# A mixture-of-experts layer with cross attention: another order of the first rows' work, and the second v and W of later rows between gate products

## The chip, the cores and the metric

One core of one Trainium2 chip runs the kernel. The metric is the device time of one execution in microseconds; the time before is the median of three runs. TensorE's granted clock was full (1.0) throughout the profiled execution.

## The reference

Eight batch rows of 512 tokens with 256 channels, and for each a context of 64 tokens. All is float32.

```python
nx = _layer_norm(x, ln_gamma, ln_beta)
q = nx @ Wq
k = prototype_bank @ Wk
v = prototype_bank @ Wv
scores = jnp.einsum('bth,bph->btp', q, k) * H ** (-0.5)
weights = jax.nn.softmax(scores, axis=-1)
evidence = jnp.einsum('btp,bph->bth', weights, v)
combined = jnp.concatenate([nx, evidence, anchor], axis=-1)
router_probs = jax.nn.softmax(combined @ router_W + router_b, axis=-1)
h = jax.nn.silu(jnp.einsum('btc,ecr->bter', combined, e_w1) + e_b1)
expert_out = jnp.einsum('bter,erh->bteh', h, e_w2) + e_b2
routed = jnp.sum(expert_out * router_probs[..., None], axis=-2)
g = jax.nn.sigmoid(jax.nn.silu(combined @ gate_w1 + gate_b1) @ gate_w2 + gate_b2)
return x + g * (routed @ out_w + out_b)
```

There are three experts of 512 hidden channels; `anchor` is one vector for each batch row.

## The kernel before

The batch rows are taken in four pairs, j = 0 to 3. For a pair the kernel runs `gate_layer`, then `expert_layer` for e = 0, 1, 2, then `outputs`. The text calls pair 0 "the first rows". The order of all instructions on every engine is the order in which the program writes them (`manual_schedule`); semaphores between engines follow from who reads and writes which tile.

**Seven products for eight.** The two batch rows of a pair, the two halves of the 256 input channels and neighbouring chunks of 128 output channels make 2x2 block products, which are done with seven products (`nx_product`, which = 1 to 7) over sums and differences of the blocks. The differences of the weights (`ws`, called sums in the text) are made once on GpSimd: `combine_weights(g)` is four adds or subtracts (L233 to L236) for expert g, with g = E for the gate. The differences of x (t1 to t4) are made by `combine_x` (L640). Products are accumulated in PSUM banks U, Y and Z, with L792 as the line of all of them; partial results are copied out by ScalarE (`keep_part`, L834) and added by VectorE (`add`, L831). A product that accumulates in U can start only when the copy before it has read U.

**Evidence.** The context part of `combined` is not formed. `value_weights(j, g)` multiplies v with the middle third of expert g's first weights ("v and W", `vw`, four matmuls at L767, a copy at L774), and `evidence` multiplies the turned softmax weights `wT` with it, as two streams on the two halves of the array. `value_differences` (L781) subtracts neighbouring chunks of `vw` for one of the two batch rows. Expert 0 and the gate need theirs at the end of `gate_layer`; expert 1's ("the second v and W") is used at the end of expert 0's layer.

**PSUM.** Eight banks. The small jobs take theirs from a list in turn (`misc`, set by `spares`): before the loop banks 4, 6, 7, in `gate_layer` 7 and 5. A bank is free again when what was in it has been read.

**The first rows.** Before the loop the program lists one by one: context and weights turned, v, keys joined with queries (`project(wkqT, ...)`, copied by `keep_m`, L360 and L361), x normalized and turned by TensorE (`transpose_x`, scaled on the way out by VectorE L566 for the first half of the channels and by ScalarE L570 for the second), the scores (L649), the softmax (L659 to L686: transposed, maximum, subtract, exp, sum, reciprocal, multiply), and `turn_weights` (L693, L695). `anchor_rows(g)` multiplies the anchors with the last third of the weights; `anchor_columns` adds the biases later. `load_table` runs a dummy activation, so that the table of a function is loaded at that place in ScalarE's queue.

**GpSimd's queue** carries, besides the sums, DMAs of the router: `store_router_rows` (two stores to `vrd`), `store_router_anchor` (`rbd`, from `scr_k`), `spread_router_bias` (two loads of `rbd`, L407), `spread_router_rows` (two loads of `vrd`, L423), and `router_column` (two multiplies or subtracts, L402 and L403). SyncE's queue loads all weights, in order; `load_second(0)` (L475) is the load of the first expert's second weights into a buffer that held `rrow`, the source of the `rbd` store.

**Later rows.** While `outputs(j)` runs its long products (`experts`), steps for pair j + 1 are put between them, by the dictionary `between`; those for a layer itself are in `within`. The points are names: P2, P7, P3 and so on lie between two calls of `experts`, "gate" between products 3 and 7 of `gate_layer`, (0, "S") after the first silus of expert 0's layer, (0, "A"), (0, "B"), (0, "C"), (0, "D") further down in it.

Of the kernel before, what the change touches and what calls it, by code (L numbers as in the profile page):

```python
# [9 lines left out]
AF = mybir.ActivationFunctionType  # L10
# [6 lines left out]
def kernel(  # L17
# [100 lines left out]
    def load_table(func):  # L118
        nc.scalar.activation(warm_t, warm_t, func)
# [254 lines left out]
    def router_anchor():  # L374
        ps = misc("ps_rb")
        for k in range(KH):
            nc.tensor.matmul(
                ps[:ED, :B], rwd[:, 2 * KH + k, :], condT[:, k, :B], start=(k == 0), stop=False
            )
        for k in range(KH):  # L380

            nc.tensor.matmul(
                ps[:ED, :B], rw2[:, k, :ED], beta_c[:, k : k + 1].to_broadcast([P, B]),
                start=False, stop=(k == KH - 1),
            )
        dst = rrow.rearrange("e (i j) -> e j i", i=2)
        src = ps[:ED, :B].rearrange("e (j i) -> e j i", i=2)
        nc.scalar.activation(dst, src, AF.Identity, bias=rb_c[:, 0:1])
# [253 lines left out]
    def scores(j):  # L642


        ps = misc(f"ps_s_{j}")
        for g in range(2):
            for k in range(KH):
                for i, h in SIDES:
                    nc.tensor.matmul(  # L649
                        ps[side(i, h), g * NH : (g + 1) * NH],  # L650
                        mr[:, k, 2 * j + i, g * TB : (g + 1) * TB],
                        S["nxT", 2 * j + i][:, k, h * NH : (h + 1) * NH],
                        start=(k == 0),
                        stop=(k == KH - 1),
                    )
        w = work.tile([P, 2, NJ, TB], F32, tag="w", name=f"w_{j}", bufs=1)
        S["w", j] = w
        tokens = w.rearrange("p g j c -> p j g c")
        nc.vector.transpose(w.rearrange("p g j c -> p (g j c)"), ps)  # L659
        nc.vector.tensor_copy(logits(j)[:, 1, :], w[:, 0, :, 0])  # L660
        nc.vector.memset(w[:, 0, :, 0], 0.0)
        mx = work.tile([P, NJ], F32, tag="mx", name=f"mx_{j}")
        nc.vector.tensor_reduce(mx, tokens, AX.XY, ALU.max)
        sm = work.tile([P, NJ], F32, tag="sm", name=f"sm_{j}")
        S["sm", j] = sm
        if j == 0:
            nc.vector.tensor_tensor(w, w, by_token(mx), ALU.subtract)
            nc.scalar.activation(w, w, AF.Exp, scale=SCALE)
            nc.vector.tensor_reduce(sm, tokens, AX.XY, ALU.add)
            return  # L670
        nmx = work.tile([P, NJ], F32, tag="nmx", name=f"nmx_{j}")
        nc.vector.tensor_scalar_mul(nmx, mx, -SCALE)
        for t in range(NJ):
            nc.scalar.activation(
                w[:, :, t, :], w[:, :, t, :], AF.Exp, bias=nmx[:, t : t + 1], scale=SCALE,
                accum_out=sm[:, t : t + 1],
            )

    def by_token(a):
        return a.unsqueeze(1).unsqueeze(3).to_broadcast([P, 2, NJ, TB])  # L680
# [527 lines left out]
    with tc.manual_schedule(engines=None):  # L1208
# [33 lines left out]
        load_table(AF.Exp)  # L1242
        project(wkqT, ctxT, keep_m, "m")
        router_anchor()
        value_weights(0, E)
        store_router_rows(0)
        store_router_anchor()
        combine_weights(E)
        transpose_x(1)
        combine_x(0, nc.vector, (0, 1))  # L1250
        scores(0)
        load_table(AF.Silu)
        combine_weights(0)
        router_column()
        spread_router_bias()
        spread_router_rows(0)
        softmax(0)
        value_weights(0, 0, nc.vector.tensor_copy)
        anchor_rows(E)
        anchor_rows(0)  # L1260
        combine_x(0, nc.vector, (2,))
        turn_weights(0)
        combine_weights(1)
        late_scratch()
        load_anchor(1)
        load_anchor(2)
# [4 lines left out]
        for j in range(NP):  # L1271


            within, between = {}, {}

            def put(where, n, step, *args):
                where.setdefault(n, []).append(lambda: step(*args))

            if j == 0:
                put(within, "gate", value_weights, 0, 1)  # L1280
                put(within, (0, "S"), combine_x, 0, nc.vector, (3,))
                put(within, (0, "S"), router_part, 0)
                put(within, (0, "A"), router_part, 1)
                put(within, (0, "A"), load_x, 2)
                put(within, (0, "A"), load_x, 3)
                put(within, (0, "B"), combine_weights, 2)
                put(within, (0, "B"), combine_gate)
                put(within, (0, "A"), anchor_rows, 1)
                put(within, (0, "A"), router_logits, 0)
                put(within, (0, "A"), load_second, 1)  # L1290
                put(within, (0, "C"), transpose_second, 0)
                put(within, (0, "C"), anchor_columns, 1)
                put(within, (0, "C"), anchor_rows, 2)
                put(within, (0, "C"), second_bias)
                put(within, (0, "C"), router_exp, 0)
                put(within, (0, "D"), router, 0)
                put(within, (0, "C"), load_second, 2)
                put(within, (0, "D"), second_layer, 0)
                put(within, (0, "D"), spread_probabilities, 0)
                put(within, (0, "D"), combine_second, 0)  # L1300
                put(within, (1, "A"), transpose_second, 1)
                put(within, (1, "B"), second_layer, 1)
                put(within, (1, "B"), combine_second, 1)
                put(within, (1, "C"), transpose_second, 2)
                put(within, (1, "C"), anchor_columns, 2)
                put(within, (1, "D"), second_layer, 2)
                put(within, (1, "D"), combine_second, 2)
            if j:
                put(within, (0, "S"), router, j)
                put(within, (0, "S"), spread_probabilities, j)  # L1310
            if j and j + 1 < NP:
                put(within, (0, "B"), statistics, 2 * j + 3, 0, NT)
            put(within, (0, "C" if j == 0 else "B"), value_weights, j, 2)
            put(within, (1, "C"), load_x_blocks, 2 * j)
            put(within, (2, "A"), gate_differences, j)
            put(within, (2, "C"), load_x_blocks, 2 * j + 1)
            if j + 1 < NP:
                b0, b1 = 2 * j + 2, 2 * j + 3
                if j + 2 < NP:
                    put(between, "begin", load_x, b0 + 2)  # L1320
                    put(between, "begin", load_x, b1 + 2)
                put(within, (0, "A" if j else "D"), statistics, b0, 0, NT)
                if j == 0:
                    put(within, (0, "D"), statistics, b1, 0, NT)
                for i in range(2):
                    put(within, (0, "D") if j else (1, "S"), deviation, j + 1, i)
                for b in (b0, b1):
                    put(within, (1, "W" if j else "S"), normalize, b)
                    put(within, (1, "W" if j else "S"), store_x, b)
                put(within, (1, "C"), regroup_x, b0)  # L1330
                put(within, (1, "A" if j else "B"), router_part, b0)
                put(within, (1, "D" if j else "B"), router_part, b1)
                put(between, "begin", transpose_blocks, b0)
                put(between, "gate", regroup_x, b1)
                put(between, "begin", value_weights, j + 1, E)
                put(between, "begin", store_router_rows, j + 1)
                put(between, "begin", spread_router_rows, j + 1)
                put(between, "P5", transpose_blocks, b1)
                put(between, "P2", scores, j + 1)
                put(between, "P2", combine_x, j + 1, nc.gpsimd)  # L1340
                put(between, "P7", softmax, j + 1)
                put(between, "P7", value_weights, j + 1, 0)
                put(between, "P7", router_logits, j + 1)
                put(between, "P3", value_weights, j + 1, 1)
                put(between, "P3", turn_weights, j + 1)
                put(between, "P3", router_exp, j + 1)
            gate_layer(j, within)
            for e in range(E):
                expert_layer(j, e, within)
            outputs(j, between)  # L1350
# [34 lines left out]
```

## Time and profile before

| | us |
|---|---|
| median of 3 runs (lowest, highest) | 465.32 (464.8, 465.38) |
| the profiled execution, its own time | 465.82 |
| its span, first to last instruction | 463.7 |
| TensorE busy | 458.4 |
| VectorE busy | 365.9 |
| ScalarE busy | 214.3 |
| GpSimd busy | 101.0 |

A row of a timeline has: start in us from the span's start, time in us (of all instructions of the row, if there are several), engine, line, operation, what it writes and reads, shape, count, and in brackets the idle time of the engine before it with what ended it. PE is TensorE's matmul, PEld its weight load, DVE VectorE, ACT ScalarE, POOL GpSimd, SPq SyncE's queue. A row of the chain of waits in order of time has start, time, engine, tile and line. The ends of matmuls are modelled, so matmul starts are the safer numbers. A row of the waits has who waited, for whom, total us, times, longest.

### The profile page before, as it was taken

The numbers are of one execution on the slowest core, as the hardware profiler recorded it, in microseconds if no ns is written. First come the engines' busy times: TensorE is split into PE (matmuls) and PEld (weight loads), VectorE is DVE, ScalarE is ACT, GpSimd is POOL, SyncE is SP. The second block draws the span as 40 slices with busy tenths as digits, with TensorE's granted clock in tenths as the row PEclk, the third lists the DMA queues.
The fourth block names the chain that finished last, engine by engine and source line by source line (L and its number), as shares of the span: only waits on it lengthen the run. The fifth ranks groups of instructions, "written<-read, shape, count | busy, mean of one in ns | idle before, by whom it ended". The sixth has DMA issues, their size and how long they took to land.

```text
span 463.7 us, 4758 instructions
## 1 busy us (share of the span) xinstructions
PE 458.4 (99%) x1457; PEld 210.0 (45%) x1457; DVE 365.9 (79%) x683; ACT 214.3 (46%) x370; POOL 101.0 (22%) x149
## 2 busy tenths in 40 slices
PE   9999999999999999999999999999999999999996
PEld 7534555444444444444444444444444444444455
DVE  2898878969799659879799659978889625797983
ACT  3435583656222566557221576458230455458000
POOL 6475614101081300001072300001062300000020
PEclk9999999999999999999999999999999999999999
DMA  8983677402012325812011334702011480000014
GB/s 280 371 167 102 100 234 114 98 0 45 7 23 39 65 104 128 149 41 46 6 24 23 46 136 107 112 9 46 6 24 23 70 205 0 0 0 1 0 19 72
DMA packets 119401, 35.26 MB, mean 76 GB/s; under 512 B 106045, under 2 KB 116337, under 8 KB 118865
## 3 DMA queue, kind: packets, MB, share of 16 engines
q1 hardware_dynamic: 115168, 26.95, 28.7%
q0 software_dynamic: 2176, 7.17, 4.7%
q10 hardware_dynamic: 2032, 0.85, 0.7%
q8 instruction: 11, 0.18, 0.2%
q14 instruction: 14, 0.11, 0.1%
HBM read 27.56 MB, written 7.39 MB: 75 GB/s over the span
## 4 chain that ended last, share of the span: by engine, by line
PE 93%; DVE 6%; issue 0%; ACT 0%
PE ps_u L792 42%; PE ps_z L792 18%; PE ps_y L792 13%; PE ps_vw L767 5%; PE ps_gu L792 3%; PE ps_w2o L501 2%; PE ps_s L649 2%; PE ps_gz L792 1%; DVE h L1068 1%; PE ps_tokens L792 1%; PE ps_wake L294 1%; DVE h L876 1%; PE ps_v L339 1%; PE ps_m L339 1%; PE ps_gy L792 1%; DVE r L1078 0%
## 5 line engine op out<-in xcount | busy, mean ns | idle before, releaser
L876 DVE TENSOR_TENSOR h<-h,pb 128x512 f32<-128x512 f32 x96 | 62.0, 696 | 6.5 <-ACT h L825 6.5
L792 PE MATMUL ps_u<-h,w2o 128*128 128x512 f32 x144 | 64.1, 594 | 0.0
L792 PE MATMUL ps_u<-nxT,w 128*128 128x512 f32 x112 | 55.5, 606 | 0.0
L825 ACT ACTIVATE h<-h,abias 128x512 f32<-128x512 f32 x72 | 49.6, 719 | 12.5 <-DVE h L831 12.0
L1101 POOL TENSOR_TENSOR yb<-yb,xb 128x512 f32<-128x512 f32 x14 | 18.4, 1318 | 145.5 <-DVE yb L1100 128.2
L792 PE MATMUL ps_z<-wT,vw 64*128 64x512 f32 x104 | 49.5, 605 | 0.0
L792 PE MATMUL ps_z<-h,w2s 128*128 128x512 f32 x96 | 42.6, 593 | 0.2 <-DVE r L1084 0.2
L792 PEld LDWEIGHTS ps_u<-h,w2o 128*128 128x128 f32 x144 | 27.0, 190 | 32.5 <-issue 29.7
L834 ACT COPY h<-ps_u 128x512 f32<-128x512 f32 x48 | 28.0, 582 | 29.7 <-PE ps_u L792 29.4
L415 POOL DMA_DIRECT2D vrd<-vw x8 | 5.0, 629 | 137.1 <-ACT vw L774 137.1
L1068 DVE TENSOR_TENSOR h<-h,h 128x1024 f32<-128x1024 f32 x24 | 34.4, 1487 | 0.0
L792 PEld LDWEIGHTS ps_u<-nxT,w 128*128 128x128 f32 x112 | 19.9, 189 | 30.1 <-issue 25.6
L825 ACT ACTIVATE h<-ps_u,abias 128x512 f32<-128x512 f32 x24 | 16.5, 687 | 29.7 <-PE ps_z L792 29.4
L831 DVE TENSOR_TENSOR h<-h,ps_y 128x512 f32<-128x512 f32 x24 | 16.4, 683 | 17.2 <-PE ps_y L792 15.7
L792 PEld LDWEIGHTS ps_z<-h,w2s 128*128 128x128 f32 x96 | 18.1, 190 | 23.5 <-issue 21.8
L792 PE MATMUL ps_z<-T,ws 128*128 128x512 f32 x56 | 28.6, 592 | 0.0
L792 PE MATMUL ps_y<-nxT,w 128*128 128x512 f32 x56 | 28.6, 592 | 0.0
L792 PE MATMUL ps_u<-wT,vw 64*128 64x512 f32 x56 | 27.9, 613 | 0.5 <-DVE hg L831 0.5
L831 DVE TENSOR_TENSOR h<-h,ps_z 128x512 f32<-128x512 f32 x24 | 16.2, 685 | 14.2 <-PE ps_z L792 14.1
L792 PE MATMUL ps_y<-wT,vw 64*128 64x512 f32 x56 | 27.0, 596 | 0.0
L767 PE MATMUL ps_vw<-w,vT 128*128 128x512 f32 (+1 forms) x64 | 27.0, 544 | 0.0
L792 PE MATMUL ps_u<-T,ws 128*128 128x512 f32 x56 | 26.8, 595 | 0.1
(236 smaller groups left out, 804.2 us busy)
## 6 DMA issues: line engine op xcount, KB each, us to landing
pb<-pd POOLq DMA_DIRECT2D x4, 1536.0 KB, 6.4
xb<-in_x_dram SPq DMA_DIRECT2D x64, 64.0 KB, 2.5
out_dram<-yb SPq DMA_DIRECT2D x56, 64.0 KB, 2.0
w<-in_L_xcond_e_w_dram SPq DMA_DIRECT2D x6, 512.0 KB, 10.3
x<-in_x_dram SPq DMA_DIRECT2D x24, 128.0 KB, 3.0
xd<-x SPq DMA_DIRECT2D x24, 128.0 KB, 2.4
xg<-xd SPq DMA_DIRECT2D x48, 64.0 KB, 2.4
scr_wa<-in_L_xcond_e_w_dram SPq DMA_DIRECT2D x3, 512.0 KB, 16.6
```

The lines of the kernel that those rows point to most:

```text
L339: nc.tensor.matmul(ps, w_sb[:, k, m * P : (m + 1) * P], src[:, k, :], start=(k == 0), stop=(k == KH - 1))
L415: nc.gpsimd.dma_start(S["vrd", j][i].rearrange("e c -> c e"), S["vw", j][row_half(i), R0:])
L501: nc.tensor.matmul(ps[:, d * H : (d + 1) * H], w2T[:, k, (i + d) * P : (i + d + 1) * P], ow_sb[:, k, :], start=(k == 0), stop=(k == KH - 1),)
L649: nc.tensor.matmul(ps[side(i, h), g * NH : (g + 1) * NH], mr[:, k, 2 * j + i, g * TB : (g + 1) * TB], S["nxT", 2 * j + i][:, k, h * NH : ( ...
L767: nc.tensor.matmul(ps, vT[:, k, j * 2 * CT : (j + 1) * 2 * CT], w1[:, KH + k, n0:n1], start=(k == 0), stop=(k == KH - 1),)
L792: nc.tensor.matmul(ps, lhsT, rhs, start=start, stop=True, skip_group_check=not start)
L825: nc.scalar.activation(h, h if src is None else src, AF.Silu, bias=abias[:, c, 2 * j + i : 2 * j + i + 1])
L831: nc.vector.tensor_tensor(h, h, part, ALU.add)
L834: nc.scalar.copy(chunk(n, i, d), part)
L876: nc.vector.tensor_tensor(h, h, S["pb", j][:, i, :, 2 * q // RC, :], ALU.mult)
L1068: nc.vector.tensor_tensor(d, p, m, ALU.subtract)
L1101: nc.gpsimd.tensor_tensor(yb, yb, S["xb", 2 * j + row][:, i, :], ALU.add)
```

## The change

In the first rows:

- x of the second batch row is turned before the gate's v and W is multiplied, instead of after it.
- The sum over the exponentials becomes a step of its own (`sum_weights`), which stands after the anchor rows.
- The first v and W is copied by ScalarE instead of VectorE, and its difference follows after the softmax.
- The load of the Silu table moves from behind the scores to the "gate" point, behind the second v and W.
- On GpSimd, `router_column` and `spread_router_bias` go ahead of `combine_weights(0)`, and `combine_weights(1)` moves from before the loop to point (0, "B") of the first expert layer.
- The second v and W's difference moves from the "gate" point to (0, "S").

In the later rows the second v and W moves from point P3 of the outputs before to the "gate" point between products 3 and 7, and its difference to (0, "S").

```diff
@@ scores
             nc.scalar.activation(w, w, AF.Exp, scale=SCALE)
-            nc.vector.tensor_reduce(sm, tokens, AX.XY, ALU.add)
             return
@@ new
+    def sum_weights(j):
+        nc.vector.tensor_reduce(
+            S["sm", j], S["w", j].rearrange("p g j c -> p j g c"), AX.XY, ALU.add
+        )
@@ before the loop
         router_anchor()
+        transpose_x(1)
         value_weights(0, E)
         store_router_rows(0)
         store_router_anchor()
         combine_weights(E)
-        transpose_x(1)
         combine_x(0, nc.vector, (0, 1))
         scores(0)
-        load_table(AF.Silu)
-        combine_weights(0)
         router_column()
         spread_router_bias()
+        combine_weights(0)
         spread_router_rows(0)
-        softmax(0)
-        value_weights(0, 0, nc.vector.tensor_copy)
+        value_weights(0, 0, nc.scalar.copy, False)
         anchor_rows(E)
         anchor_rows(0)
+        sum_weights(0)
+        softmax(0)
+        value_differences(0, 0)
         combine_x(0, nc.vector, (2,))
         turn_weights(0)
-        combine_weights(1)
         late_scratch()
@@ in the loop, j == 0
-                put(within, "gate", value_weights, 0, 1)
+                put(within, "gate", value_weights, 0, 1, nc.scalar.copy, False)
+                put(within, "gate", load_table, AF.Silu)
                 put(within, (0, "S"), combine_x, 0, nc.vector, (3,))
+                put(within, (0, "S"), value_differences, 0, 1)
                 put(within, (0, "S"), router_part, 0)
...
+                put(within, (0, "B"), combine_weights, 1)
                 put(within, (0, "B"), combine_weights, 2)
@@ in the loop, j > 0
             if j:
+                put(within, "gate", value_weights, j, 1, nc.scalar.copy, False)
+                put(within, (0, "S"), value_differences, j, 1)
                 put(within, (0, "S"), router, j)
...
                 put(between, "P7", router_logits, j + 1)
-                put(between, "P3", value_weights, j + 1, 1)
                 put(between, "P3", turn_weights, j + 1)
```

## The prediction

> **What bounds the kernel now.** I read the busy shares first, then the chain of waits, then the timeline of the first 37 us and of the start of the second pair of rows.
>
> ```profile
> PE 458.4 (99%) x1457; PEld 210.0 (45%) x1457; DVE 365.9 (79%) x683; ACT 214.3 (46%) x370; POOL 101.0 (22%) x149
> ...
> PE 93%; DVE 6%; issue 0%; ACT 0%
> ```
>
> TensorE carries 93% of the chain that ended last. So an edit pays only where it closes a gap between two products. In the chain in order of time a product of 512 columns (two instructions) takes 0.86 us and the four of a v-times-W product take 1.72:
>
> ```profile
> 43.98 0.86 PE ps_y L792 x2
> ...
> 132.95 1.72 PE ps_vw L767 x4
> ```
>
> With those two prices I compared each stretch with what it would take without gaps. After 37 us almost nothing is left except the steps between tile shapes (about 0.1 us each, in every pair of rows). The gaps that this change can reach lie in four places.
>
> Scores of the first rows. L649 begins at 19.63; its second rows' part waits until VectorE has written the turned x (L566, end 20.11), a loss of 0.08 us:
>
> ```profile
> 18.32 0.68 DVE L361 TENSOR_TENSOR mr<-ps_m,scr_small 128x504 f32<-128x504 f32 x1
> 19.30 0.81 DVE L566 TENSOR_SCALAR nxT<-pt_x,cols 128x512 f32<-128x512 f32 x1 [0.30 <-PE pt_x L579]
> 19.63 2.46 PE L649 MATMUL ps_s<-nxT,mr 128*32 128x256 f32 x32
> 20.17 0.16 PEld L649 LDWEIGHTS ps_s<-nxT,mr 128*32 128x32 f32 x8 [0.39 <-DVE nxT L566]
> ```
>
> First gate layer. The table load keeps ScalarE until 26.98, so its copy out of U ends at 27.55 and product 6, which adds to U, starts at 27.70:
>
> ```profile
> 24.73 1.12 PE L792 MATMUL ps_u<-nxT,w 128*128 128x512 f32 x2
> 25.58 1.28 ACT L119 ACT_TABLE_LOAD   x1
> 26.98 0.57 ACT L834 COPY hg<-ps_u 128x512 f32<-128x512 f32 x1
> 27.67 0.30 PEld L792 LDWEIGHTS ps_u<-T,ws 128*128 128x128 f32 x2 [0.92 <-POOL w L235]
> ```
>
> The row names L235, but that ended at 26.98 and belongs to another expert's sums; what ended just before is the copy. From 24.73 to the first evidence product at 32.16 are 7.43 us. Six products and one v-times-W are 6x0.86+1.72 = 6.88, and two shape steps 0.19: 7.07. **Gap 0.36.**
>
> First evidence. The last turning of the softmax weights ends at 32.51, so the two half-array streams run out of step; then the next evidence product needs U, and the sum that reads U (L831) queues behind the difference of the second v and W (L781):
>
> ```profile
> 32.16 0.69 PE L792 MATMUL ps_y<-wT,vw 64*128 64x512 f32 x1
> 33.34 0.91 DVE L781 TENSOR_TENSOR vw<-vw 64x256 f32<-64x256 f32 x1
> 34.28 0.69 DVE L831 TENSOR_TENSOR hg<-hg,ps_u 128x512 f32<-128x512 f32 x1
> 35.02 0.18 PEld L792 LDWEIGHTS ps_u<-wT,vw 64*128 64x128 f32 x1 [1.31 <-DVE hg L831]
> 36.94 1.12 PE L792 MATMUL ps_u<-nxT,w 128*128 128x512 f32 x2
> ```
>
> The same stretch of the second rows, and the fourth gap ahead of it:
>
> ```profile
> 146.52 1.02 PE L792 MATMUL ps_u<-nxT,w 128*128 128x512 f32 x2
> 150.16 0.59 ACT L834 COPY hg<-ps_u 128x512 f32<-128x512 f32 x1 [1.08 <-PE ps_u L792]
> 150.89 1.10 PE L792 MATMUL ps_u<-nxT,w 128*128 128x512 f32 x2
> 151.91 0.69 PE L792 MATMUL ps_y<-wT,vw 64*128 64x512 f32 x1
> 155.55 1.12 PE L792 MATMUL ps_u<-nxT,w 128*128 128x512 f32 x2
> ```
>
> Evidence takes 151.91 to 155.55 = 3.64 there and 32.16 to 36.94 = 4.78 in the first rows: **gap 1.14.** And the later gate takes 146.52 to 151.91 = 5.39, where six products and one step are 5.16+0.09 = 5.25: **gap 0.14**, since product 7 adds to U and its copy (150.16 to 150.75) is only just done. It is the same 5.39 from 252.56 and from 358.6.
>
> **The change part by part.**
>
> x turned ahead of the gate's v and W. Same eight transposes and four matmuls, swapped; x is normalized at 17.22 and TensorE comes at 17.69, so no wait there. But the shared banks go round 4, 6, 7. Before, the scores got bank 6 from the gate's v and W, read by ScalarE at 19.24. Now they get it from the first half of the turned x, and must wait for L566 to read it. VectorE is busy to 19.00 with L361, so L566 runs 19.02 to 19.83 and the scores start at about 19.89 instead of 19.63: 0.26 lost, and the 0.08 wait inside goes: **+0.18.** Bounds: -0.08 (no bank wait) to +0.3. The gate's v and W is copied at 19.73 instead of 18.86, so GpSimd's two vrd stores, its rbd store and the gate's four sums all move 0.87 later. The first sum was ready at 21.92, product 5 needs it at 25.9: covered by 3 us.
>
> Other order of copies, table load. ScalarE now does: exp (24.93+0.18 = 25.11 to 25.74), the first v and W's copy (0.59, taken from VectorE, where it was 0.68), the copy of U (26.35 to 26.92). Product 6's weights are due at about 27.16: 0.24 spare, the gap of 0.36 closes. **-0.36**, bounds -0.36 to 0. The Silu table (1.28 in the row) follows the second v and W's copy at 31.8, ends with its dummy activation at 33.2; the first silu needs the Y sum, as in the second rows 1.89 us after evidence starts, 33.87. Nothing but that silu queues behind it. The Trainium skill, "ScalarE: Activation LUTs", section "Step-by-step: what each stage is for", gives about 2.7 us including the drain: then silu slips by 0.75, and ScalarE's next copy for TensorE, 1.33 before its old 38.10, still has 1.4 us. By either price 0; the row is taken.
>
> VectorE's chain to the softmax weights. Work now between exp and the evidence: sum 0.69, reciprocal 0.20, product 0.69, difference 0.42, third x difference 0.69, turning 0.70+4x0.44. The 0.68 copy is gone and the two anchor turnings (0.45) fit under exp. Starting at 25.78 the chain ends near 31.0; evidence is due at 24.91+7.07 = 31.98. So 0.9 spare. Next on VectorE are the anchor columns and the U sum, about 32.05 to 32.75; TensorE returns to U at 31.98+1.82 = 33.8. L781 now stands after evidence, in a place where VectorE idled 1.5 us before L831 at 40.73; its result is due near 55.6 (56.95-1.33). **-1.14**, bounds -1.14 to -0.5 (streams out of step and a late U sum again).
>
> A rule against this: the Trainium skill, "SBUF — State Buffer", section "Who interferes with whom", says that a VectorE instruction with two SBUF inputs and a GpSimd instruction that reads SBUF block each other wholly. The rows show part of it: L781 takes 0.72 and 0.91 beside GpSimd's sums, 0.42 elsewhere. If expert 0's sums fell on this chain, the rows make it about 1.0 longer (0.1 us of stall), full blocking by three adds of 0.73 about 2.2 (1.3 of stall). I expect neither, since GpSimd should stand idle then, for this reason:
>
> ```profile
> SPq L475 <- DMA rbd<-scr_k: 11.1, 1, 11.1
> ...
> 30.35 1.11 POOL L407 DMA_DIRECT2D rbias<-rbd  x2 [0.88 <-DMA rbd<-scr_k]
> ```
>
> GpSimd's order. The store of rbd, issued at 20.76, landed at 30.07 behind the weight loads. The bias spread (L407) now stands before expert 0's four sums, so these wait for that landing: landing about 31 (0.87 later), spread to 32.3, sums to 35.4, rows' spread (L423) to 36.5, landing 3 later. TensorE needs the first sum at 40.48-1.33 = 39.1, VectorE the rows at 43.32-1.33 = 42.0. Hidden by 6 and 2.5 us: 0. SyncE's load of e_w2 waits for the same landing; used at 48.77, it lands near 37. Expert 1's sums move behind router_part's copies, to about 44.5 to 47.5; due at 63.4. Expert 2's and the gate's sums then end near 52, where the probabilities' store (52.91) was next: at most 0.1 late, and the pb it feeds landed at 62.97, used at 74.89.
>
> Later rows. The second v and W (1.72 of TensorE, a 0.59 copy, a 0.42 difference) leaves the stretch at 139.82 and stands between products 3 and 7. TensorE's sum is equal. It covers U's copy: **-0.14 x 3 = -0.43**, bounds -0.43 to +0.3 (a new wait of 0.1 each). Its bank is 7, last read at 128.5. Where it left, the last expert products start 1.72 earlier; their bank was read by 136.74, needed at 139.8. Its ScalarE copy ends at 151.6, before table load and silu (153.80). The difference delays the probabilities by 0.42; pb lands 4.0 us ahead of its use even in the last rows (381.07, 385.08).
>
> **Sum:** +0.18-0.36-1.14-0.43 = -1.75. Does it last? After 37 us VectorE waits for TensorE again and again (1.11 at 58.15, 0.76 at 66.97, 2.12 at 100.60), so its chains move along. The profiled execution took 465.82 around a span of 463.7; the span becomes 461.95, and the median of the runs 465.32-1.75 = 463.57.
>
> **The rivals.** (1) Half the first rows' gain: chain late or GpSimd in its way, 0.7 back: 464.3. For it: margins of 0.24, 0.9 and 1.0 us, worked out from rows of another order. (2) More: no bank wait, -2.0: 463.3. (3) No change that counts: the first rows come to wait for something with a time of its own, a DMA, and the later gap just moves: 464.9. Against it: all loads that the next stages use landed long before. (4) Slower, by one mechanism: the rbd landing L. Rows' spread lands at L+7.9 (1.4 spread, 3.0 sums, 0.5 and 3.0); VectorE needs it at 42.0, and behind it stand the turnings of e_w2, which have 1.2 us before TensorE wants them (50.06, 51.26). TensorE stalls by L-35.3. From L = 37 the gain is gone, from 38 it is slower by over 0.9; at L = 40.5, 468.8. L was 30.07 and moves with the last weight loads (32.2): not likely.
>
> **How the numbers follow.** The forecast 0.58 (range of its own 463.0 to 464.2), (1) 0.14, (2) 0.10, (3) 0.12, (4) 0.06. 0.2% is 0.93 us, about what a measurement here can tell. Faster by more: 0.58+0.14+0.10 = 0.82; within 0.12; slower 0.06. The range, from below (2) to just under (3): 462.9 to 464.9.
>
> **What would show it.** Scores starting near 19.9 with L566 as releaser; product 6 directly after product 2; evidence 3.6 to 3.7 long; the later gates without the hole before product 7; GpSimd idle until rbd lands. Wrong: a VectorE wait at L705 for vr, a gap at evidence's U, or the span unchanged while the first 37 us are shorter.

## The result and the profile after

The changed kernel takes **463.56 us** (median of 6 runs, 463.34 to 464.38), the kernel before on the same chip 465.49 (6 runs, 464.8 to 465.85). The ratio is 0.9961, with a 95% interval of 0.9949 to 0.9974. Against the 465.32 from which the prediction was made that is -1.76 us, against the runs beside it -1.93.

The profiled execution took 463.56 around a span of 461.4; that of before took 465.82 around 463.7. So the spans differ by 2.27 us (463.72 to 461.45), more than the medians do. The experiments return to that.

New lines push those behind the scores down: L792 of before is L796, L831 is L835, L834 is L838, L774 is L778, L781 is L785, L767 is L771, L686 is L690, L693 and L695 are L697 and L699, L669 is L679.

The page after, busy times with their share of the span, and the chain of work that ended last:

```profile
PE 456.7 (99%) x1457; PEld 210.5 (46%) x1457; DVE 364.7 (79%) x682; ACT 214.8 (47%) x371; POOL 100.0 (22%) x149
...
PE 95%; DVE 4%; issue 0%
```

The chain gained two points of TensorE and lost two of VectorE. Where that is can be seen in the chain in order of time, from 17 to 40 us (start, time, engine, tile, line). Before, the chain left TensorE when the scores ended and ran through VectorE's softmax and turnings up to the evidence. Now every piece in this stretch is TensorE's:

```profile
19.93 1.87 PE ps_s L649 x32
...
31.57 0.62 PE ps_y L796
...
35.21 2.77 PE ps_u L796 x6
```

The timeline of the changed kernel, first at the scores, then the first gate layer, then the evidence:

```profile
19.01 0.80 DVE L566 TENSOR_SCALAR nxT<-pt_x,cols 128x512 f32<-128x512 f32 x1
19.86 1.45 PEld L649 LDWEIGHTS ps_s<-nxT,mr 128*32 128x32 f32 x32 [0.34 <-DVE nxT L566]
19.86 1.93 PE L649 MATMUL ps_s<-nxT,mr 128*32 128x256 f32 x32
21.73 1.98 PE L771 MATMUL ps_vw<-w,vT 128*128 128x512 f32 x4
...
24.44 1.13 PE L796 MATMUL ps_u<-nxT,w 128*128 128x512 f32 x2
25.83 0.59 ACT L838 COPY hg<-ps_u 128x512 f32<-128x512 f32 x1
26.26 1.02 PE L796 MATMUL ps_y<-nxT,w 128*128 128x512 f32 x2
27.12 1.02 PE L796 MATMUL ps_u<-T,ws 128*128 128x512 f32 x2
...
28.95 1.80 DVE L699 STREAM_TRANSPOSE wT<-w 32x256 f32<-32x256 f32 x4
31.36 1.28 ACT L119 ACT_TABLE_LOAD   x1
31.50 0.69 PE L796 MATMUL ps_y<-wT,vw 64*128 64x512 f32 x1
31.51 0.69 PE L796 MATMUL ps_z<-wT,vw 64*128 64x512 f32 x1
31.61 0.69 DVE L835 TENSOR_TENSOR hg<-hg,ps_u 128x512 f32<-128x512 f32 x1 [0.55 <-PE ps_u L796]
33.39 0.72 ACT L829 ACTIVATE hg<-hg,abias 128x512 f32<-128x512 f32 x1 [0.54 <-DVE hg L835]
35.14 1.13 PE L796 MATMUL ps_u<-nxT,w 128*128 128x512 f32 x2
```

- The scores start later than before and yet end earlier: 1.86 us in place of 2.39. The row names L566 as what they waited for, but that ended at 19.81, and the same idle time of 0.34 us ahead of the weights stands in a kernel whose scores wait for no bank (under "The turned x"). TensorE came 0.28 later in this execution.
- The rows at 26.26 and 27.12 are products 2 and 6. They are 0.86 apart, the length of a product: no hole is left.
- The turning of the softmax weights ends at 30.75, the evidence starts at 31.50. Its two half-array streams start 0.01 apart, in step. The sum that reads U ends at 32.30, a microsecond before TensorE writes U again.

In starts of TensorE, before and after, the stretches are:

| stretch of the first rows | before | after | difference |
|---|---|---|---|
| scores, to the first v and W | 19.63 to 22.02 | 19.86 to 21.73 | 2.39 to 1.86 |
| gate, to the evidence | 24.73 to 32.16: 7.42 | 24.44 to 31.50: 7.07 | -0.36 |
| evidence, to expert 0 | 32.16 to 36.94: 4.78 | 31.50 to 35.14: 3.63 | -1.15 |

(Differences are taken from starts with more digits than the rows show.) In the second rows of the changed kernel the timeline now has the second v and W between products 3 and 7:

```profile
146.63 0.58 ACT L838 COPY hg<-ps_u 128x512 f32<-128x512 f32 x1 [1.08 <-PE ps_u L796]
147.29 1.88 PE L771 MATMUL ps_vw<-w,vT 128*128 128x512 f32 x4
149.01 1.02 PE L796 MATMUL ps_u<-nxT,w 128*128 128x512 f32 x2
149.96 0.69 PE L796 MATMUL ps_y<-wT,vw 64*128 64x512 f32 x1
```

The gate takes 143.00 to 149.96 = 6.96. Less the 1.72 of the v and W that came into it, that is 5.24, where it took 5.39: -0.15 in each of three pairs. U's copy (146.63 to 147.21) is done 1.8 us before product 7 at 149.01.

GpSimd's part of the timeline:

```profile
31.16 1.11 POOL L407 DMA_DIRECT2D rbias<-rbd  x2 [5.09 <-DMA rbd<-scr_k]
...
34.97 1.04 POOL L423 DMA_DIRECT2D vr<-vrd  x2
...
52.01 2.03 POOL L751 DMA_DIRECT2D pd<-prT  x4 [0.87 <-DVE prT L748]
```

GpSimd idles for 5.09 us until the rbd store has landed, with VectorE's whole chain in that time. Everything behind it is later and nothing waits for it: the probabilities' store leaves at 52.01, and left at 52.91 before.

### The profile page after: what moved, and what is told of

Same layout as the page of the kernel before. It is cut to its first block, busy times and chain, and to the rows that moved or that the text cites. A ratio compares the mean times of both kernels' runs of the same rounds, so it can differ in the third digit from the quotient of the medians.

```text
span 461.4 us, 4756 instructions
## 1 busy us (share of the span) xinstructions
PE 456.7 (99%) x1457; PEld 210.5 (46%) x1457; DVE 364.7 (79%) x682; ACT 214.8 (47%) x371; POOL 100.0 (22%) x149
## 4 chain that ended last, share of the span: by engine, by line
PE 95%; DVE 4%; issue 0%
PE ps_u L796 43%; PE ps_z L796 18%; PE ps_y L796 14%; PE ps_vw L771 5%; PE ps_gu L796 3%; PE ps_w2o L501 2%; PE ps_s L649 2%; PE ps_gz L796 1%; DVE h L1072 1%; PE ps_tokens L796 1%; PE ps_wake L294 1%; DVE h L880 1%; PE ps_v L339 1%; PE ps_m L339 1%; PE ps_gy L796 1%; DVE r L1082 0%
## 5 line engine op out<-in xcount | busy, mean ns | idle before, releaser
L796 PE MATMUL ps_u<-h,w2o 128*128 128x512 f32 x144 | 64.1, 595 | 0.0
L796 PE MATMUL ps_u<-nxT,w 128*128 128x512 f32 x112 | 55.3, 604 | 0.0
L796 PE MATMUL ps_z<-wT,vw 64*128 64x512 f32 x104 | 49.5, 605 | 0.0
L796 PE MATMUL ps_z<-h,w2s 128*128 128x512 f32 x96 | 42.6, 593 | 0.2 <-DVE r L1088 0.2
L838 ACT COPY h<-ps_u 128x512 f32<-128x512 f32 x48 | 27.9, 582 | 30.2 <-PE ps_u L796 29.8
L796 PEld LDWEIGHTS ps_u<-h,w2o 128*128 128x128 f32 x144 | 27.0, 190 | 32.5 <-issue 29.4
L1072 DVE TENSOR_TENSOR h<-h,h 128x1024 f32<-128x1024 f32 x24 | 34.3, 1482 | 0.0
L796 PEld LDWEIGHTS ps_u<-nxT,w 128*128 128x128 f32 x112 | 20.2, 190 | 29.4 <-issue 24.2
L796 PEld LDWEIGHTS ps_z<-h,w2s 128*128 128x128 f32 x96 | 18.2, 190 | 23.5 <-issue 21.8
L796 PE MATMUL ps_z<-T,ws 128*128 128x512 f32 x56 | 28.6, 592 | 0.0
L796 PE MATMUL ps_y<-nxT,w 128*128 128x512 f32 x56 | 28.6, 592 | 0.0
L835 DVE TENSOR_TENSOR h<-h,ps_y 128x512 f32<-128x512 f32 x24 | 16.4, 683 | 15.0 <-PE ps_y L796 14.0
L796 PE MATMUL ps_u<-wT,vw 64*128 64x512 f32 x56 | 27.8, 612 | 0.0
L796 PE MATMUL ps_y<-wT,vw 64*128 64x512 f32 x56 | 27.0, 597 | 0.0
L771 PE MATMUL ps_vw<-w,vT 128*128 128x512 f32 (+1 forms) x64 | 26.9, 543 | 0.0
L796 PE MATMUL ps_u<-T,ws 128*128 128x512 f32 x56 | 26.7, 594 | 0.0
L835 DVE TENSOR_TENSOR h<-h,ps_z 128x512 f32<-128x512 f32 x24 | 16.2, 684 | 13.3 <-PE ps_z L796 13.2
```

Source lines behind the costliest of these rows:

```text
L771: nc.tensor.matmul(ps, vT[:, k, j * 2 * CT : (j + 1) * 2 * CT], w1[:, KH + k, n0:n1], start=(k == 0), stop=(k == KH - 1),)
L796: nc.tensor.matmul(ps, lhsT, rhs, start=start, stop=True, skip_group_check=not start)
L835: nc.vector.tensor_tensor(h, h, part, ALU.add)
L838: nc.scalar.copy(chunk(n, i, d), part)
L1072: nc.vector.tensor_tensor(d, p, m, ALU.subtract)
```

## The experiments

The theory is the prediction's: four gaps in TensorE's stream, each closed by an edit of its own. The rivals are that other edits did it (the moved difference, the moved sums), that the scores' part loses rather than gains (as the prediction has it), and that the later rows' part gives nothing.

### The two halves of the change

Later rows alone, on the kernel before:

```diff
             if j:
+                put(within, "gate", value_weights, j, 1, nc.scalar.copy, False)
+                put(within, (0, "S"), value_differences, j, 1)
                 put(within, (0, "S"), router, j)
@@
-                put(between, "P3", value_weights, j + 1, 1)
```

> The kernel before with the later rows' part alone. Theory (the v and W covers ScalarE's copy out of U): each later gate loses its hole before product 7, so that from first gate product to evidence it takes 5.25 + 1.72 = 6.97 us, the span is 0.43 shorter (463.3 if the first rows stay at 36.94) and the first rows keep their 7.43 and 4.78. Rival (the later gain only came because the first rows shifted everything): the later gates take 7.1 and more, or the span stays within 0.1 of before.

464.87 (12 runs, 463.93 to 465.53) against 465.01: ratio 0.9994, interval 0.9984 to 1.0003. By time alone this can't be told from nothing. The trace tells it: the later gates take 6.96, of which 1.72 is the v and W, and from expert 0 to the end are 426.32 us instead of 426.78, **-0.46**. The first rows are those of before (evidence 4.66).

First rows alone, from the changed kernel with those lines taken back:

> The changed kernel with the later rows' part taken back. Theory (parts add up): expert 0 of the first rows starts at 35.1, 1.8 earlier than before; the later gates have their old 5.39; the span is 461.4 + 0.43 = 461.8 to 461.9. Rival (first rows' gain is eaten later without the other part): span over 462.5.

464.06 (12 runs, 463.96 to 464.25) against 465.01: ratio 0.9978 (0.9969 to 0.9986). Expert 0 starts at 35.07 (before 36.94), and from there to the end are 426.80 us, as before. So in the traces the first rows' gain reaches the end whole, and the two parts add: -1.87 here and -0.46 there make 2.33 of span, where the change as a whole has 2.27. By the runs they are -0.95 and -0.14: the medians of before lie lower than its trace.

### The turned x

The turning back behind the gate's v and W:

```diff
         router_anchor()
-        transpose_x(1)
         value_weights(0, E)
@@
         combine_weights(E)
+        transpose_x(1)
         combine_x(0, nc.vector, (0, 1))
```

> The changed kernel with x turned after the gate's v and W again. Theory (the scores lost about 0.5 inside, waiting for both halves of the turned x; turning x earlier has them ready): the scores take 2.3 to 2.4 instead of 1.87 and start about 0.2 earlier, the gate's start moves from 24.4 to 24.7, the span is 0.3 longer. Rival (the recorded sum: x turned earlier costs 0.18 because of the bank that the scores get): the gate starts 0.2 earlier, the span is 0.2 shorter.

463.68 (463.37 to 464.25), span 461.84 instead of 461.45; the time is within the spread of the changed kernel's runs, the trace is clear. The timeline of this kernel at the scores:

```profile
19.70 0.14 PEld L649 LDWEIGHTS ps_s<-nxT,mr 128*32 128x32 f32 x4 [0.17 <-issue]
19.70 2.46 PE L649 MATMUL ps_s<-nxT,mr 128*32 128x256 f32 x32
20.24 0.16 PEld L649 LDWEIGHTS ps_s<-nxT,mr 128*32 128x32 f32 x8 [0.40 <-DVE nxT L566]
...
22.09 0.30 PEld L771 LDWEIGHTS ps_vw<-w,vT 128*128 128x128 f32 x2 [0.41 <-issue]
```

With the scores begun before all of x is turned, they take 22.09 - 19.70 = 2.39; begun when all is ready, 1.86. Only four of the 32 weight loads come before the wait for L566. From the first one after it, at 20.24, to the end are 1.85 us, as long as a whole group takes with all ready. So the early start gained nothing here: the 0.54 between 19.70 and 20.24 is lost whole.

How much of this the kernel keeps depends on when TensorE arrives at the router's anchor, which differs by execution (17.15 to 17.70). From there to the first v and W are 4.60 to 4.61 us in the order of before, in the traces of before, of this kernel, and of the two built on before that leave the scores as they were; 4.04 in the new order when TensorE comes at 17.69, and up to 4.47 when it comes at 17.15, because the scores then stand until 19.73 or later for L566 to read their bank. In these traces the new order wins 0.1 to 0.6.

Which of the two halves of the turned x goes to which engine, changed for the second batch row, so that the scores' bank is freed by ScalarE:

```diff
-            scale_x(S["nxT", b][:, k, :], k, pt, k % 2 == 0)
+            scale_x(S["nxT", b][:, k, :], k, pt, k % 2 == b)
```

> The changed kernel with ScalarE scaling the first half of the second turned x and VectorE the second half (in the changed kernel the other way round). Theory (the scores wait until 19.8 for VectorE to read the bank that they get, and VectorE is held until 19.0 by the keys' differences): the bank is free at about 19.4, the scores start at about 19.6 and the wait for the second half is hidden behind the first: scores end 0.2 to 0.25 earlier, span 461.2. Rival (the wait moves inside the scores): scores start at 19.6 but take 2.1, span 461.4.

463.5 (463.17 to 463.97). The timeline of this kernel:

```profile
19.67 1.45 PEld L649 LDWEIGHTS ps_s<-nxT,mr 128*32 128x32 f32 x32 [0.34 <-issue]
```

The scores start 2.17 us after the anchor with no wait for a bank, and take 1.86. In the profile of the changed kernel it was also 2.17, so the bank cost nothing there. With the engines not swapped and TensorE coming between 17.15 and 17.27, it was 2.51 to 2.61. In this execution TensorE came at 17.50, so the edit was worth little. The last experiment, with the same edit, has TensorE at 17.20, and there it shows.

### ScalarE's order

The Silu table's load back behind the scores:

```diff
         scores(0)
+        load_table(AF.Silu)
         router_column()
@@
-                put(within, "gate", load_table, AF.Silu)
```

> The changed kernel with the Silu table load behind the exponential again. Theory (ScalarE's queue decides when U is free for product 6): table 1.28 and dummy activation come before the copies, U's copy ends near 28.0 instead of 26.4, product 6 starts about 1.0 late; gate stretch 8.0 to 8.2 instead of 7.06, span 1.0 longer, 462.4. Rival (some other wait follows anyway and hides it): gate stretch under 7.5.

464.64 (20 runs, 464.13 to 464.78) against 464.95: ratio 0.9987 (0.998 to 0.9993), a microsecond above the changed kernel. The timeline of this kernel in the gate:

```profile
25.48 1.28 ACT L119 ACT_TABLE_LOAD   x1
...
26.89 0.57 ACT L778 COPY vw<-ps_vw 128x512 f32<-128x512 f32 x1
27.35 0.59 ACT L838 COPY hg<-ps_u 128x512 f32<-128x512 f32 x1
28.08 1.10 PE L796 MATMUL ps_u<-T,ws 128*128 128x512 f32 x2 [0.80 <-ACT hg L838]
```

The gate takes 8.10 instead of 7.07: **+1.03**. The copy of U ends at 27.94 and product 6 starts at 28.08; it would have started at 27.12. The two edits of this step belong together: to give ScalarE the copy of v and W without taking the table load away costs more (8.10) than leaving both as they were (7.42).

The first v and W copied by VectorE instead, at its new place:

```diff
-        value_weights(0, 0, nc.scalar.copy, False)
+        value_weights(0, 0, nc.vector.tensor_copy, False)
```

> The changed kernel with the first v and W copied by VectorE again (at its new place in the order). Theory (there is 0.75 between the end of the softmax weights' turning and evidence): the copy, 0.68, falls partly under the exponential, the chain ends about 0.4 later, 31.1 against 31.5: gate 7.06, evidence 3.63, span the same. Rival (the copy's engine is what brought the evidence into step): evidence 3.9 or more, span 0.3 to 0.7 longer.

463.54 (463.46 to 463.73): no cost. The copy falls in the time in which VectorE waits for the exponentials, so its chain still ends early, at 30.40 against evidence at 31.37. Which engine makes this copy is not what matters; when it stands there is.

### What closed the gap at the evidence

The second v and W's difference back in the gate layer:

```diff
-                put(within, "gate", value_weights, 0, 1, nc.scalar.copy, False)
+                put(within, "gate", value_weights, 0, 1)
@@
-                put(within, (0, "S"), value_differences, 0, 1)
```

> The changed kernel with the second v and W's difference at the gate again, in front of the U sum on VectorE. Theory A (the chain to the softmax weights was late, and the difference was only the last in it): VectorE is now 1.3 us earlier, the difference runs at about 31.4 to 31.8 and the U sum ends by 32.6, before TensorE needs U at 33.3: evidence stays at 3.64, span the same within 0.1. Theory B (the difference in front of the sum was the stall): evidence 4.2 or more, span 0.5 longer.

463.62 (463.56 to 463.86); the evidence takes 3.63. The difference (0.42, at 31.26) moves the sum that reads U to 31.71 to 32.40, and TensorE writes U again at 33.2. With the chain early, this move does nothing.

The same move alone, on the kernel before:

```diff
-                put(within, "gate", value_weights, 0, 1)
+                put(within, "gate", value_weights, 0, 1, nc.scalar.copy, False)
                 put(within, (0, "S"), combine_x, 0, nc.vector, (3,))
+                put(within, (0, "S"), value_differences, 0, 1)
```

> The kernel before with only the second v and W's difference of the first rows moved behind evidence. Theory (of the 1.14 us in evidence, 0.64 to 0.74 were the U sum behind the difference and 0.4 the half streams out of step): gate stays 7.43, evidence 4.0 to 4.15, span 463.0. Rival (the chain alone decides): evidence 4.6 or more.

465.06 (12 runs, 464.65 to 465.48) against 465.12: ratio 0.9999 (0.9989 to 1.0008), no gain that can be measured. Its trace, though, has an evidence of 3.69. The timeline of this kernel says why:

```profile
26.40 0.69 DVE L686 TENSOR_TENSOR w<-w,rs 128x512 f32<-128x512 f32 x1
...
28.36 0.64 POOL L233 TENSOR_TENSOR ws<-w 128x256 f32<-128x256 f32 x1 [5.23 <-DMA w<-in_L_xcond_e_w_dram]
...
30.20 1.80 DVE L695 STREAM_TRANSPOSE wT<-w 32x256 f32<-32x256 f32 x4
32.00 0.69 PE L792 MATMUL ps_y<-wT,vw 64*128 64x512 f32 x1
32.06 0.69 PE L792 MATMUL ps_z<-wT,vw 64*128 64x512 f32 x1
```

The same of before:

```profile
24.86 0.64 POOL L233 TENSOR_TENSOR ws<-w 128x256 f32<-128x256 f32 x1 [1.57 <-DMA w<-in_L_xcond_e_w_dram]
...
26.26 0.72 POOL L235 TENSOR_TENSOR w<-w 128x256 f32<-128x256 f32 x1
26.55 0.97 DVE L686 TENSOR_TENSOR w<-w,rs 128x512 f32<-128x512 f32 x1
...
30.70 1.80 DVE L695 STREAM_TRANSPOSE wT<-w 32x256 f32<-32x256 f32 x4
```

GpSimd's sums for expert 0 start 0.07 us after the last of the six loads of the experts' first weights has landed (expert 0's own landed by 15.5). That load landed at 24.79 in the profile of before and at 28.29 here, though nothing ahead of it was changed. So GpSimd was idle while VectorE made most of its chain, the product took 0.69 and not more, and the chain ended at 32.00, just as the evidence starts. In the profile of before the sums fell on the chain and it ended at 32.51.

This trace mixes the moved difference with the late landing. By an estimate the landing did most: the sum that reads U ends at 33.45 here, with the difference (0.42) in front it would end near 33.87, and TensorE writes U at 33.82. So the old place of the difference would have cost about 0.1. **The gap of 1.14 us thus hangs on a landing, and need not be in every execution of the kernel before.** In the 14 traces this load landed between 24.55 and 25.05 in twelve, at 28.29 here and at 29.39 with x turned back. What the moved difference is worth with an early landing, no trace shows.

The order on VectorE of before, on the changed kernel:

```diff
-        value_weights(0, 0, nc.scalar.copy, False)
-        anchor_rows(E)
-        anchor_rows(0)
         sum_weights(0)
         softmax(0)
-        value_differences(0, 0)
+        value_weights(0, 0, nc.vector.tensor_copy)
+        anchor_rows(E)
+        anchor_rows(0)
         combine_x(0, nc.vector, (2,))
```

> The changed kernel with VectorE's order between exponential and turning as before (sum, softmax, then the first v and W's copy on VectorE and its difference, then the anchors' turnings); ScalarE's table, GpSimd's order and the second difference stay changed. Theory (the order as a whole brought the chain forward, each piece alone hides in its margin): the chain ends about 31.9, 0.4 after TensorE is due at 31.5; gate 7.06, evidence 4.0 to 4.1, span 0.4 longer, 461.8. Rival (the stall in evidence was only the U sum): evidence 3.63.

463.98 (15 runs, 463.55 to 464.11), ratio 0.9977 (0.9969 to 0.9985). By these runs the old order costs the expected 0.4: the variant with expert 1's sums back, which equals the changed kernel where it counts, had 463.54 on the same chip. The traced execution shows less. Its evidence takes 3.73, a tenth lost. The timeline of this kernel:

```profile
29.71 1.80 DVE L699 STREAM_TRANSPOSE wT<-w 32x256 f32<-32x256 f32 x4
...
31.46 0.69 PE L796 MATMUL ps_y<-wT,vw 64*128 64x512 f32 x1
31.57 0.69 PE L796 MATMUL ps_z<-wT,vw 64*128 64x512 f32 x1
```

The chain ends at 31.51, 0.05 after the evidence could start, and the second stream starts 0.11 behind the first. GpSimd idles until 30.72, so no sum slows the chain. From the sum over the exponentials the old order takes 6.32 us (25.19 to 31.51), the new one 5.26 (25.49 to 30.75 in the changed kernel): 1.06 longer, which in this execution uses up the margin and hardly more. This execution (463.75) is one of the five fastest; the other ten took 463.86 to 464.11, and where they lose the rest was not traced.

Expert 0's sums on GpSimd back ahead of the router's column:

```diff
         scores(0)
+        combine_weights(0)
         router_column()
         spread_router_bias()
-        combine_weights(0)
```

> The changed kernel with expert 0's four sums ahead of the router column on GpSimd again, so beside VectorE's softmax chain. Theory by the rows (operations with two inputs from SBUF slow from 0.42 to 0.7 or 0.9 and from 0.69 to about 1.0 beside GpSimd's sums): chain 0.3 to 1.0 later than 30.75, so 0 to 0.25 of stall, span 461.4 to 461.7. By the rule that the two block each other wholly: chain 1.5 to 2.2 later, 0.8 to 1.4 of stall, span 462.2 to 462.8. Rival (GpSimd's order does not touch this chain): VectorE's durations as in the changed kernel.

463.36 (463.26 to 463.58): no cost, but this is where the weighed rule can be read. VectorE's and GpSimd's timeline in this kernel:

```profile
25.61 0.73 POOL L234 TENSOR_TENSOR ws<-ws,w 128x256 f32<-128x256 f32 x1
26.00 0.89 DVE L690 TENSOR_TENSOR w<-w,rs 128x512 f32<-128x512 f32 x1
26.29 1.18 POOL L235 TENSOR_TENSOR w<-w 128x256 f32<-128x256 f32 x1
26.92 0.83 DVE L785 TENSOR_TENSOR vw<-vw 64x256 f32<-64x256 f32 x1
27.43 0.82 POOL L236 TENSOR_TENSOR ws<-w,ws 128x256 f32<-128x256 f32 x1
27.76 1.03 DVE L640 TENSOR_TENSOR nxT<-nxT 128x512 f32<-128x512 f32 x1
...
29.45 1.80 DVE L699 STREAM_TRANSPOSE wT<-w 32x256 f32<-32x256 f32 x4
```

Beside the sums, the product takes 0.89 (0.69 elsewhere), the difference 0.83 (0.42), the third x difference 1.03 (0.69): 0.95 in all. The chain ends at 31.25, 0.14 before the evidence (31.39). In size this is the prediction's estimate from rows (about 1.0 longer). But the rows fit the rule that it had set against that, the exclusive lock of the Trainium skill's "SBUF — State Buffer", "Who interferes with whom". Each of the three operations ends when the add that was running at its start has ended, plus its own time alone, less 0.14:

- product: 26.34 (end of L234) + 0.69 - 0.14 = 26.89, as in its row;
- difference: 27.47 (end of L235) + 0.42 - 0.14 = 27.75, as in its row;
- x difference: 28.25 (end of L236) + 0.69 - 0.14 = 28.80, against 28.79.

The adds wait in the same way: L235, 0.73 alone, ends at 26.89 + 0.73 - 0.14 = 27.48 (27.47 in its row). In the profile of before the product ends at 26.98 (end of L235) + 0.69 - 0.14 = 27.53, against 27.52. In the 14 traces, all 36 operations on VectorE of these two shapes, with both inputs in SBUF, that began during one of GpSimd's adds between 17 and 60 us end within 0.01 of this sum. So the two engines take turns. The prediction's 2.2 for the lock was too large because it let every operation wait for a whole add; each waits for the rest of one, here 0.20, 0.41 and 0.34.

So each of the two causes of the long chain, the old order on VectorE (1.06) and the sums beside it (0.95), costs little at the evidence alone: 0.1 and 0 in these traces, though the runs charge 0.4 for the old order. In the profile of before both were there. Its product took 0.97 and its first difference 0.72, beside the sums, which is 0.58 of waiting; 5.26+1.06+0.58 = 6.90 is the length of its chain (25.60 to 32.51). Without the waiting it would have ended at 31.93 by this sum, ahead of the evidence at 32.16.

### What was moved on GpSimd

Expert 1's sums back to before the loop:

```diff
         turn_weights(0)
+        combine_weights(1)
         late_scratch()
@@
-                put(within, (0, "B"), combine_weights, 1)
```

> The changed kernel with expert 1's sums before the loop again, so behind the rows' spread on GpSimd, about 36 to 39. Theory (this move costs and brings nothing: VectorE has slack at that place): all first-row stretches and the span as in the changed kernel, 461.3 to 461.5, though VectorE's products for the router (0.42) go slower beside the sums. Rival (the move takes GpSimd out of VectorE's way where it counts): span 0.2 or more longer, with a gap on TensorE between 36 and 42.

463.54 (463.45 to 463.69), span 461.36: nothing, as expected.

### A version that beats both

Two holes were left in the trace of the changed kernel: the bank that holds the scores when TensorE is early, and one in the last outputs, where a product waits for VectorE to read its bank. The timeline of the changed kernel there:

```profile
432.78 2.35 DVE L1072 TENSOR_TENSOR h<-h,h 128x1024 f32<-128x1024 f32 x2
435.05 0.68 DVE L1088 TENSOR_TENSOR r<-r,ps_z 128x512 f32<-128x512 f32 x1
435.78 2.41 PE L796 MATMUL ps_z<-h,w2s 128*128 128x512 f32 x5 [0.19 <-DVE r L1088]
```

The sum that frees bank Z stands behind a group of long differences (L1072, of which the row shows the last two). The version has the swapped engines and, in the last outputs only, puts this sum ahead of the second group:

```diff
-            scale_x(S["nxT", b][:, k, :], k, pt, k % 2 == 0)
+            scale_x(S["nxT", b][:, k, :], k, pt, k % 2 == b)
@@
         subtract((0, 1), ((1, 1), (0, 1)))
+        if j + 1 == NP:
+            keep(r22, z)
         subtract((0, 0), ((0, 1), (0, 0)))
-        keep(r22, z)
+        if j + 1 < NP:
+            keep(r22, z)
```

> The changed kernel with the engines of the second turned x swapped (as in the earlier experiment) and, in the last outputs alone, the sum that reads the z bank put ahead of the second group of differences on VectorE. In the changed kernel the first z product of the last seventh waits until 435.78 for that sum, 0.36 and 0.10 of refill. Theory: that gap closes, the span is 0.46 shorter than with the swap alone, 460.8; median about 463.0. Rival (the differences, now 0.7 later, are missed by a product): the gap moves to a later product and the span stays at 461.2.

**462.80** (6 runs, 462.58 to 463.37), ratio 0.9958 (0.9945 to 0.9971), where the variant with expert 1's sums back, which equals the changed kernel where it counts, had 463.54 on the same chip: -0.74. Its timeline:

```profile
19.38 1.93 PE L649 MATMUL ps_s<-nxT,mr 128*32 128x256 f32 x32
...
434.95 3.60 PE L796 MATMUL ps_z<-h,w2s 128*128 128x512 f32 x8
```

The scores start 2.18 after TensorE's arrival at 17.20, where with the bank held they started at 19.73 or later for the same arrival: some 0.35. The product into Z starts at 434.95 with no wait. The span is 460.50.

## Why the prediction was right, step by step

The time (463.57 told, 463.56 measured) is closer than the steps deserve; that the figures agree to 0.01 is luck. The step for the scores had the wrong sign, and the step for the evidence was taken from one execution; the two errors point in opposite ways.

**Scores: failed.** The step "+0.18" was made of 0.26 lost to the bank and 0.08 won inside. The first half held in number only: the start was 19.86 (told 19.89), but TensorE came 0.28 later in this execution, and with 2.17 from there the bank cost nothing. Where TensorE came at 17.15 to 17.27, the bank's wait was there, 0.34 to 0.44 of it (2.51 to 2.61 against 2.17). The second half was mis-sized: the group had not 0.08 to win but 0.53, since its early start was worth nothing. Measured: the scores end at 21.73 instead of 22.02, **-0.29**, in spite of the later arrival. The number was to be had: later rows' scores, with all operands ready, take 1.86 in the trace of before.

**Gate: right.** Told -0.36, measured -0.36 (7.42 to 7.07); U's copy told as 26.35 to 26.92, was 25.83 to 26.42, since the exponentials and the first v and W's copy came earlier with the scores. The spare of 0.24 told for it was about 0.27 to the weight load at 26.69. With the table load back the step costs 1.03: the load is what closed it.

**Evidence: size right, scope wrong.** Told -1.14, measured -1.15 between the two profiles (4.78 to 3.63), chain end told 31.0, was 30.75. But the gap is that of the profiled execution. Moving the difference alone gave an execution with 3.69, in which by the estimate above the landing did most, and no timed gain. So the step subtracted from a median a stall that need not be in every run. The term for the lock in the forecast's weighing (2.2, with 1.3 of stall) was too large, as shown; as the sums no longer fell on the chain, it did not enter the time.

**Later rows: right.** Told -0.14 each, measured -0.15 each, -0.46 together in the kernel with that part alone.

**The sum.** In spans: -0.29-0.36-1.15-0.47 = -2.27, as the spans say, against the -1.75 told. By medians it is -1.76 and -1.93; the variants that cost nothing have -1.4 to -1.6 against the runs of before beside them. The difference lies with before: its profiled execution, 465.82, is above its medians. The 33 runs of before beside the last experiments fall into two groups, 14 from 464.27 to 464.64 and 19 from 465.02 to 466.43, with medians of 464.42 and 465.62, 1.2 apart. Beside the other experiments the division is weaker (27 runs with a hole from 464.97 to 465.34) or absent (29 runs). The runs of the changed kernel and of its variants spread over 0.2 to 1.0.

Two other things vary between the traces: TensorE's arrival at the anchor (17.15 to 17.70) and the end after the last product (3.5 or 3.7). Before's trace, at 17.41 and 3.5, would come to about 465.56 by an estimate with the earliest arrival, so these two alone do not make a run of 464.4. That the lower group is the one without the evidence's stall fits in size (1.2 beside 1.14). It was not shown: no execution of that group was traced, and the late landing was seen in 2 of 14 traces, where 14 of 33 runs are in the group.

**Hidden work: right.** The Silu table after the second v and W costs nothing: the silu at 33.39 waits for VectorE's sum. The load took 1.28 as in the rows; the 2.7 that the prediction had weighed, from the Trainium skill's "ScalarE: Activation LUTs", "Step-by-step: what each stage is for", appears in no trace here. GpSimd idled until rbd landed (told about 31, was 30.87), bias spread, sums to 35.0 (told 35.4), rows' spread to 36.0 (told 36.5), expert 1's sums 43.75 to 46.5 (told 44.5 to 47.5), the end of all sums at 51.1 (told 52): nothing waits for any of it.

**The rivals.** Of (1), a part may have come true in another place: the median shows less of the first rows' gain than the trace, but the changed kernel's chain was not late. (2), -2.0 with no bank wait, described the trace better than the forecast did: the bank cost nothing in it, though only because TensorE came late. (3): what the stages wait for has no time of its own; the chain from 17 to 40 us has TensorE alone. (4): L was 30.87, six microseconds under the break-even of 37.

## What to carry to other kernels

Price a group of small products by the same group elsewhere with its operands ready, not by the one wait that its rows show. Before a stall goes into a sum against a median, ask whether it holds in every execution: if it hangs on when a bulk load lands, the profile has one draw of it. A stall can need two causes, so that each alone hides in a margin. When work moves on an engine, give what is due first (here the copy of U) the place ahead of what nothing waits for (the table load).

## What was not expected of the hardware

- 32 score matmuls on four column tiles of 32 took 2.39 us when some of their operands came 0.54 us after the start, and 1.86 with all ready, in every trace. From the first weights after the wait they still took 1.85.
- The same weight load, behind the same transfers, let GpSimd start at 24.86, 24.89, 24.99 and 28.36 us in four executions.
- Operations of VectorE with two inputs in SBUF took 1.3 to 2.2 times as long beside GpSimd's adds (0.69 to 0.89 and 1.03; 0.42 to 0.83 and 0.91), and the adds up to 1.6 times (0.73 to 1.18). The rows show turns: end of the other engine's instruction, plus one's own time, less 0.14.
